# The end of an attention stage: the last batch's maxima in three further rounds, its sums in two parts, and eight units of the output projection in attention's PSUM banks

## The chip, the core and the metric

The kernel runs on one core of one Trainium2 chip, as one launch. The metric is the device time of that launch in microseconds, the median of several executions. Lower is better.

Five engines work side by side, each with its own queue of instructions taken in order: TensorE (PE in the profile, with PEld for its weight loads), VectorE (DVE), ScalarE (ACT), GpSimd (POOL) and SyncE (SP), which here only issues DMAs. All data is float32.

## The reference

Four sub-layers run one after the other over 8 batches of 512 tokens of 256 channels: a sparse attention, a routed feed-forward net, a gated linear attention with its own feed-forward net, and the routed net again. Each is added to its input. The change touches the first only:

```python
q = _split_heads(x @ Wq + bq)          # 16 heads of 16 channels
k = _split_heads(x @ Wk + bk)
v = _split_heads(x @ Wv + bv)
scores = jnp.einsum('bhqd,bhkd->bhqk', q, k) * scale
sparsity = scores.max(axis=-1) - scores.mean(axis=-1)
_, top_idx = jax.lax.top_k(sparsity, U)          # U = 307 of 512 queries
...
attn = jax.nn.softmax(scores_sel, axis=-1)
out_sel = jnp.einsum('bhuk,bhkd->bhud', attn, v)
out = jnp.zeros_like(q).at[bi, hi, top_idx].set(out_sel)
...
return out @ Wo + bo
```

So a query needs its maximum over all keys twice: for the softmax, and to decide whether it is among the 307 of its head whose output is kept. The other 205 give zero.

## The kernel before

**Rounds.** Attention is a loop over 128 steps: batch `b`, channel half `m`, parity `e`, query or key block `k`, 16 steps for each batch. A step handles four heads. The first pass (`max_one`) makes the scores of 128 queries against 512 keys for each of the four heads, in one PSUM bank each, and a DVE reduce (L425) takes the maxima. The second pass (`exp_one`, `weigh`) makes the same scores turned round, ACT takes the exponentials (L437), and four matmuls (L442) sum them with the values into `av`. The second pass runs `LAG = 16` steps behind the first, so in round `n` step `n` of the first pass meets step `n - 16` of the second. Rounds 112 to 127 hold the maxima of the last batch with the exponentials of batch 6; rounds 128 to 143 hold the exponentials of the last batch alone.

**Maxima.** When a group of four steps is done, `place_maxima` (L397 on) transposes and negates its maxima and sends them by eight small DMAs on SP: four into a spare row of `q` (L406), which makes the softmax subtract the maximum, and four into `neg` (L411), which collects the sparsity measure of all 128 batch-head pairs, one on each partition. `top_queries` (L464 on), called when the last maxima are in, copies `neg` into `work` and removes the 205 smallest ones: 26 turns of a DVE `max` that finds eight values and a `match_replace` that strikes them out (L471, L474).

**Sums.** `take` (L449 on) moves `av` to SBUF on ACT, sends the rows that hold the sums of the exponentials to `den` by a DMA on ACT's queue, and adds the outputs into `outC[b]` on POOL.

**The seam.** After the loop, `rden` is the reciprocal of `den` (L615) and `nrm` (L616) is `rden` where the query is kept and zero elsewhere. Sixteen small matmuls (L625) spread `nrm` over the channels of each batch and half, and sixteen DVE multiplications (L628) apply it to `outC`. Then the output projection (`out_projection`, L780) runs in units of one token block `k` and two batches: four matmuls and a DVE addition to the residual `xres` (L784), in the PSUM banks of the stage after. The four units of `k = 0` come first; the twelve others are interleaved with the ten pieces of `route(0)`: statistics of block 0 (L62, L63), a square root on ACT (L64), rows scaled by ACT (L742), their transposes (L752), the router's logits (L810, L820), its softmax and top 4, and the mask `mk`, which goes through DRAM. `routed_ffn(0)` (L904, L912, L913, L885) starts behind it and multiplies by that mask.

**Order.** Each engine's order is fixed when the program is built: a scheduler takes the instructions roughly in the order in which they are written and moves some ahead where it reckons that their inputs are there. A buffer of a pool waits until its last reader is done. The code holds an instruction back by hand with a tiny POOL copy of an element of a late result into the instruction's output (arguments named `late`).

**Banks.** Attention has 8 PSUM banks: three of pool `a_e` (`bank`), four of `a_m` (`bank_m`), one of `a_acc`.

Of the kernel before, what the change touches and what calls it, by code (L numbers as in the profile page):

```python
# [17 lines left out]
P = 128  # L18
NB = 8
# [19 lines left out]
def block_kernel(ctx: ExitStack, tc: tile.TileContext, t: dict, out: bass.AP):  # L39
# [33 lines left out]
    def load_chunked(pool, name, src, eng):  # L73

        n = src.shape[0] // P
        w = pool.tile([P, n, src.shape[1]], F32, tag=name, name=name)
        eng.dma_start(out=w, in_=src.rearrange("(c p) m -> p c m", p=P))
        return w
# [20 lines left out]
    with ExitStack() as outer:  # L99
# [20 lines left out]
        neg = a_out.tile([P, L], F32, name="neg")  # L120
        mx = a_out.tile([P, NB, NG, 4 * 4], F32, name="mx")
        work = a_out.tile([P, L + 8], F32, name="work")
        m8 = a_out.tile([P, 8], F32, name="m8")

        with ExitStack() as inner:
# [4 lines left out]
            def load_heads(name, src, eng):  # L130
                wp = load_chunked(a1, name + "_pad", src, eng)
                w = a1.tile([P, NC2, D], F32, name=name)
                nc.gpsimd.tensor_copy(
                    w.rearrange("p c (h d) -> p (c h) d", d=DH),
                    wp.rearrange("p c (h q) -> p (c h) q", q=32)[:, :, 0:DH],
                )
                return w
# [258 lines left out]
            def place_maxima(b, m, e):  # L396
# [7 lines left out]
                r = b * H + 8 * e + 4 * m  # L404
                for k in range(4):
                    nc.sync.dma_start(  # L406
                        out=q[DH * (1 - e) :: 32, m, bass.ts(k, P)],
                        in_=negT[4 * k : 4 * k + 4, :],
                    )
                for k in range(4):  # L410
                    nc.sync.dma_start(  # L411
                        out=neg[r : r + 4, bass.ts(k, P)], in_=negT[4 * k : 4 * k + 4, :]
                    )

# [49 lines left out]
            def top_queries():  # L464
# [16 lines left out]


            steps = [
                (b, g // 2, g % 2, k) for b in range(NB) for g in range(4) for k in range(4)
# [50 lines left out]
            def place_full(n):  # L535
                while full and full[0][0] <= n:
                    place_maxima(*full.pop(0)[1])

            for n in range(len(steps) + LAG + 1):
                ahead = steps[n] if n < len(steps) else None  # L540
                here = steps[n - LAG] if 0 <= n - LAG < len(steps) else None
# [26 lines left out]
                behind = (here, es) if here is not None else None  # L568
                if ahead is not None and ahead[3] == 3:
                    full.append((n + 2, ahead[0:3]))  # L570
                if n + 1 == len(steps):
                    place_full(n + 2)
                    top_queries()

# [12 lines left out]
                else:  # L587
# [7 lines left out]
                    next(pieces, None)  # L595


        wpool = ctx.enter_context(tc.tile_pool(name="wpool", bufs=1, side="right"))
# [12 lines left out]
        with tc.tile_pool(name="a_tail", bufs=2) as tail:  # L611

            nrm = tail.tile([P, L], F32, tag="nrm", name="nrm", bufs=1)
            rden = tail.tile([P, L], F32, tag="rden", name="rden", bufs=1)
            nc.vector.reciprocal(rden, den)  # L615
            nc.vector.scalar_tensor_tensor(  # L616
                nrm, work[:, 0:L][:, ::-1], REPL, rden, ALU.not_equal, ALU.mult
            )
            for u in range(2):
                for m in range(NC2):  # L620
                    for i in range(4):
                        b = 2 * i + u
                        rows = bass.ts(i, 32)
                        ps = (bank if i % 2 else bank_m)(f"nrm_ps{b}")
                        nc.tensor.matmul(  # L625
                            ps, spread[rows, u, m, :], nrm[rows, :], start=True, stop=True
                        )
                        nc.vector.tensor_tensor(  # L628
                            outC[b][:, m, :], outC[b][:, m, :], ps, ALU.mult
                        )  # L630

# [41 lines left out]
    w_down = load_chunked(wpool, "w_down", t["b_w_downT"], nc.sync)  # L673


    vm = wpool.tile([P, NC2, H], F32, name="vm")
    for c in range(NC2):
        for m in range(NC2):
            mean = vm[:, c, bass.ts(m, H // 2)]
            heads = q_w[:, c, m, 2, :].rearrange("p (h d) -> p h d", d=DH)  # L680
            nc.vector.tensor_reduce(mean, heads, AX.X, ALU.add)
            nc.vector.tensor_scalar(mean, mean, 1.0 / DH, None, ALU.mult)
            nc.vector.tensor_tensor(
                heads, heads, mean.unsqueeze(2).to_broadcast([P, H // 2, DH]), ALU.subtract
            )

# [88 lines left out]
    def out_projection(k):  # L775
# [9 lines left out]

        return [functools.partial(unit, b) for b in range(0, NB, 2)]

# [399 lines left out]
    rest = ctx.enter_context(tc.tile_pool(name="rest", bufs=1, reuse_waits="tile"))  # L1187

    bog = wpool.tile([P, NC2, P], F32, name="bog")
    ones = post.tile([P, P], F32, tag="row", name="ones", bufs=6)  # L1190
# [71 lines left out]
```

## Time and profile before

| | us |
|---|---|
| median of 3 runs (lowest to highest) | 1691.48 (1690.33 to 1694.21) |
| the profiled execution, its own time | 1690.79 |
| its span in the profile | 1689.1 |
| maxima of the last batch, rounds 112 to 127 | 481.9 to 540.6 |
| exponentials of the last batch | 541.9 to 580.3 |
| the 26 turns of `top_queries` | 549.1 to 588.8 |
| first of the spreading matmuls L625 | 593.0 |
| first matmul of the output projection L780 | 605.8 |
| first matmul of `routed_ffn(0)` L904 | 639.5 |
| first read of its mask, L913 | 650.5 |

The granted TensorE clock was 0.987 of full speed over the span. The profile has five parts that count here: busy time of each engine, the chain of work that ended last (followed back from the last instruction to what released it), groups of instructions by line with their mean duration and the idle time ahead of them, a timeline, and a table of busy time by stretches of the span. A duration in a row such as "L425 ... x512 | 328.7, 683" is a total in us and a mean in ns.

### The profile page before, as it was taken

Reading aid. Unit: us, or ns where it says so; the run is one execution under the profiler, and the core shown is the slowest. Engines: PE = TensorE matmul, PEld = TensorE weight load, DVE = VectorE, ACT = ScalarE, POOL = GpSimd, SP = SyncE. Lnnn points to the kernel's source line nnn. Section 1 sums busy time; section 2 is a strip of 40 time slices with the busy share of each in tenths; the row PEclk is TensorE's granted clock in tenths of the full one; section 3 lists DMA queues with packets and bytes.
Section 4 is the critical chain, followed back from the end, with each engine's and each line's share of the span. In section 5 each row is a group of like instructions: output and inputs, shape, how many; then the busy total and the mean of one; then the engine's idle time right before and its main releaser. Section 6 shows DMA issues by size and latency. Waiting matters only on the chain.

```text
span 1689.1 us, 19460 instructions
## 1 busy us (share of the span) xinstructions
PE 1610.8 (95%) x7298; PEld 825.8 (49%) x7298; DVE 975.3 (58%) x2007; ACT 679.7 (40%) x1215; POOL 326.9 (19%) x328
## 2 busy tenths in 40 slices
PE   7999999999999789998899989998999899999999
PEld 3423323323333166665564556545545556666766
DVE  6977777676666984437745465447264632344342
ACT  2466665666566723442253125322512353221010
POOL 3011111011001121114433242224233321000000
PEclk9999999999999989999999999999999999999999
DMA  3100000000000041100000001000000010010100
GB/s 106 39 2 3 3 2 3 2 3 2 2 3 3 24 138 26 26 13 13 0 1 1 0 0 27 0 0 1 0 0 1 1 26 0 13 39 25 48 28 25
DMA packets 23234, 27.55 MB, mean 16 GB/s; under 512 B 4932, under 2 KB 19684, under 8 KB 23140
## 3 DMA queue, kind: packets, MB, share of 16 engines
q1 hardware_dynamic: 22068, 24.74, 5.1%
q10 hardware_dynamic: 1072, 1.57, 0.3%
q8 instruction: 57, 0.93, 0.2%
q14 instruction: 37, 0.30, 0.1%
HBM read 21.19 MB, written 4.33 MB: 15 GB/s over the span
## 4 chain that ended last, share of the span: by engine, by line
PE 78%; DVE 14%; POOL 3%; ACT 2%; issue 1%; DMA 1%; SPq 0%; ACTq 0%; POOLq 0%; DVEq 0%
PE y_ps L885 16%; PE h_ps L904 12%; PE s L433 8%; PE s L422 8%; PE swi_ps L930 7%; PE av L442 7%; PE proj_ps L1012 6%; DVE pr L1044 3%; POOL o L1061 2%; DVE pr L1034 2%; PE ao_ps L780 2%; PE q_ps L316 2%; PE k_ps L316 2%; PE chT_ps L752 2%; PE gla_y L1135 2%; PE v_ps L376 2%
## 5 line engine op out<-in xcount | busy, mean ns | idle before, releaser
L425 DVE TENSOR_REDUCE mx<-s 128x1 f32<-128x512 f32 x512 | 328.7, 683 | 130.2 <-PE s L433 83.1
L437 ACT ACTIVATE e<-s 128x512 f32<-128x512 f32 x512 | 276.1, 599 | 179.1 <-PE s L433 103.5
L422 PE MATMUL s<-k,q 32*128 32x512 f32 x1024 | 299.3, 642 | 3.5 <-ACT k L367 2.8
L433 PE MATMUL s<-q,k 32*128 32x512 f32 x1024 | 294.5, 638 | 0.4 <-DVE mx L425 0.3
L885 PE MATMUL y_ps<-w,h 128*128 128x256 f32 x1024 | 233.4, 383 | 7.6 <-DVE h L913 7.6
L904 PE MATMUL h_ps<-xnT,w 128*128 128x512 f32 x512 | 231.9, 601 | 4.8 <-ACT h L912 4.8
L885 PEld LDWEIGHTS y_ps<-w,h 128*128 128x128 f32 x1024 | 193.6, 192 | 44.6 <-DVE h L913 11.0
L904 PEld LDWEIGHTS h_ps<-xnT,w 128*128 128x128 f32 x512 | 96.1, 193 | 116.1 <-issue 106.1
L442 PE MATMUL av<-e,va 128*32 128x512 f32 (+1 forms) x1120 | 142.0, 568 | 3.8 <-ACT e L437 2.4
L913 DVE TENSOR_TENSOR h<-h,mk 128x512 f32<-128x512 f32 x128 | 94.6, 751 | 84.8 <-ACT h L912 60.1
L930 PE MATMUL swi_ps<-zT,w_gate 128*128 128x512 f32 x256 | 123.1, 603 | 15.0 <-DVE h L939 15.0
L912 ACT ACTIVATE h<-h_ps,b 128x512 f32<-128x512 f32 x96 | 65.6, 685 | 171.4 <-PE h_ps L904 171.2
L930 PE MATMUL swi_ps<-zT,w_up 128*128 128x512 f32 x256 | 123.4, 603 | 10.3 <-ACT h L936 10.3
L890 DVE TENSOR_TENSOR xres<-xres,y_ps 128x512 f32<-128x512 f32 x48 | 32.9, 685 | 172.1 <-PE y_ps L885 157.8
L422 PEld LDWEIGHTS s<-k,q 32*128 32x128 f32 x1024 | 89.8, 184 | 85.8 <-DVE mx L425 55.9
L433 PEld LDWEIGHTS s<-q,k 32*128 32x128 f32 x1024 | 88.2, 183 | 80.7 <-ACT e L437 53.7
L885 PE MATMUL y_ps<-w_down,h 128*128 128x256 f32 x512 | 118.7, 384 | 2.8 <-DVE h L939 2.8
L1012 PE MATMUL proj_ps<-q_w,rT 128*128 128x512 f32 x256 | 117.0, 594 | 0.0
L885 PEld LDWEIGHTS y_ps<-w_down,h 128*128 128x128 f32 x512 | 96.8, 193 | 25.0 <-issue 9.5
L936 ACT ACTIVATE h<-swi_ps 128x512 f32<-128x512 f32 x64 | 37.9, 596 | 148.9 <-PE swi_ps L930 148.8
L1061 POOL TENSOR_TENSOR o<-o,pr 128x512 f32<-128x512 f32 (+2 forms) x56 | 84.7, 1513 | 52.5 <-DVE pr L1044 50.9
L1018 DVE TENSOR_TENSOR gate<-proj_ps,bog 128x128 f32<-128x128 f32 x64 | 18.7, 291 | 125.1 <-ACT made L1017 125.1
(189 smaller groups left out, 1752.8 us busy)
## 6 DMA issues: line engine op xcount, KB each, us to landing
mk<-md SPq DMA_DIRECT2D x32, 256.0 KB
xres<-in_L_attn_a_x SPq DMA_DIRECT2D x8, 512.0 KB
out<-xres SPq DMA_DIRECT2D x16, 256.0 KB
q<-negT SPq DMA_DIRECT2D x128, 2.0 KB
neg<-negT SPq DMA_DIRECT2D x128, 2.0 KB
w<-in_f_w1T SPq DMA_DIRECT2D x1, 1024.0 KB
w<-in_f_w2T SPq DMA_DIRECT2D x1, 1024.0 KB
w_gate<-in_b_w_gateT SPq DMA_DIRECT2D x1, 1024.0 KB
```

Of the source, the lines that this page charges most:

```text
L316: nc.tensor.matmul(ps, w[:, c, bass.ts(m, P)], xnT[:, c, :], start=(c == 0), stop=(c == NC2 - 1),)
L422: nc.tensor.matmul(s, qs[e][rows, m, bass.ts(k, P)], ks[e][rows, m, :], start=True, stop=True)
L425: nc.vector.tensor_reduce(mx[:, b, 2 * e + m, r : r + 1], s, AX.X, ALU.max)
L433: nc.tensor.matmul(s, ks[e][rows, m, bass.ts(kt, P)], qs[e][rows, m, :], start=True, stop=True)
L437: nc.scalar.activation(ex, s, AF.Exp, scale=1.0 / DH**0.5)
L442: nc.tensor.matmul(av[32 * j : 32 * j + 32, queries], va[:, 8 * kt + 4 * m + j, e, :], es[j][:, queries], start=(kt == 0), stop=(kt == 3 a ...
L885: nc.tensor.matmul(y[0][:, bass.ts(i, D)], h[f][:, bass.ts(2 * u + i, P)], w[:, f, :], start=(f == 0), stop=(f == NF - 1),)
L904: nc.tensor.matmul(ps, w1[:, c, bass.ts(f, P)], xT[g][:, c, :], start=(c == 0), stop=(c == NC2 - 1),)
L913: nc.vector.tensor_tensor(hf, hf, mk[g][:, f, :], ALU.mult)
L930: nc.tensor.matmul(ps, w[:, c, bass.ts(f, P)], zT[g][:, c, :], start=(c == 0), stop=(c == NC2 - 1),)
L1012: nc.tensor.matmul(ps, rT[b // G4][:, c, bass.ts(b % G4, P)], q_w[:, c, m], start=(c == 0), stop=(c == NC2 - 1),)
L1061: nc.gpsimd.tensor_tensor(dst, dst, src, ALU.add)
```

## The change

The maxima of the last batch are taken in rounds 112 to 124: in rounds 112, 116 and 120 a second step of the first pass runs behind the regular one, and rounds 125 to 127 have exponentials alone. For the last batch the DMAs into `neg` are issued ahead of those into `q`. `nrm` is made in two parts, first for batches 0 to 5 (96 partitions), then for 6 and 7 (32). Twelve spreading matmuls and multiplications follow the first part; then six units of the output projection for batches 0 to 5 and `k = 0, 1`; then the four spreading matmuls and multiplications of batches 6 and 7; then two units of `k = 2`. These eight units use attention's bank pool `a_e`; ACT copies their result and POOL adds it to `xres`. Eight units remain in `out_projection`, one of which is of `k = 0`. The centering of the `v` weights of the later layer (`vm`, 12 DVE instructions) is written further down. The padded `wq` and `wk` are loaded into two of the buffers that later hold `k`.

```diff
+        def weights_of(batches, late, late_form):
+            rows = slice(16 * batches[0], 16 * batches[-1] + 16)
+            first = slice(rows.start, rows.start + 1)
+            nc.gpsimd.tensor_copy(rden[first, 0:1], late)
+            nc.gpsimd.tensor_copy(nrm[first, 0:1], late_form)
+            nc.vector.reciprocal(rden[rows, :], den[rows, :])
+            nc.vector.scalar_tensor_tensor(
+                nrm[rows, :], work[rows, 0:L][:, ::-1], REPL, rden[rows, :],
+                ALU.not_equal, ALU.mult,
+            )
+
+        def weigh_outputs(batches):
+            picks = itertools.cycle((bank, bank_m))
+            for u in range(2):
+                for m in range(NC2):
+                    for b in batches[u::2]:
+                        strip = bass.ts(b // 2, 32)
+                        ps = next(picks)(f"nrm_ps{b}")
+                        nc.tensor.matmul(
+                            ps, spread[strip, u, m, :], nrm[strip, :], start=True, stop=True
+                        )
+                        nc.vector.tensor_tensor(
+                            outC[b][:, m, :], outC[b][:, m, :], ps, ALU.mult
+                        )
+
+        def out_unit(tail, k, b):
+            y = bank(f"ao_ps{b}")
+            for i in range(2):
+                for m in range(NC2):
+                    nc.tensor.matmul(
+                        y[:, bass.ts(i, D)], outC[b + i][:, m, bass.ts(k, P)],
+                        wo_a[:, m, :], start=(m == 0), stop=(m == NC2 - 1),
+                    )
+            st = tail.tile([P, L], F32, tag="ao", name=f"ao{b}")
+            nc.scalar.copy(st, y)
+            x = xres[:, b : b + 2, k, :]
+            nc.gpsimd.tensor_tensor(x, x, st.rearrange("p (b d) -> p b d", d=D), ALU.add)
...
-                wp = load_chunked(a1, name + "_pad", src, eng)
+                wp = a2.tile([P, NC2, L], F32, tag="k1", name=name + "_pad", bufs=3)
+                eng.dma_start(out=wp, in_=src.rearrange("(c p) m -> p c m", p=P))
...
+                targets = [q[DH * (1 - e) :: 32, m, :], neg[r : r + 4, :]]
+                if b == NB - 1:
+                    targets = targets[::-1]
+                for target in targets:
+                    for k in range(4):
+                        nc.sync.dma_start(
+                            out=target[:, bass.ts(k, P)], in_=negT[4 * k : 4 * k + 4, :]
+                        )
...
+            def all_maxima(step):
+                nonlocal coming
+                coming += 1
+                if step[3] == 3:
+                    full.append((n + 2, step[0:3]))
+                if coming == len(steps):
+                    place_full(n + 2)
+                    top_queries()
...
-                if ahead is not None and ahead[3] == 3:
-                    full.append((n + 2, ahead[0:3]))
-                if n + 1 == len(steps):
-                    place_full(n + 2)
-                    top_queries()
+                if here is not None:
+                    last_exps = es[3][0:1, 0:1]
+                if ahead is not None:
+                    all_maxima(ahead)
+                    if n >= 112 and n % 4 == 0 and coming < len(steps):
+                        ahead = steps[coming]
+                        for i in range(4):
+                            max_one(*ahead, i, bank_m)
+                        all_maxima(ahead)
...
+            weights_of(range(NB - 2), m8[0:1, 0:1], last_exps)
...
-            nc.vector.reciprocal(rden, den)
-            nc.vector.scalar_tensor_tensor(
-                nrm, work[:, 0:L][:, ::-1], REPL, rden, ALU.not_equal, ALU.mult
-            )
-            for u in range(2):
...
+            weigh_outputs(range(NB - 2))
+            last = outC[NB - 3][0:1, 1, 0:1]
+            weights_of(range(NB - 2, NB), last, last)
+            for k in range(2):
+                for b in range(0, NB - 2, 2):
+                    out_unit(tail, k, b)
+            weigh_outputs(range(NB - 2, NB))
+            for b in (0, 2):
+                out_unit(tail, 2, b)
...
-        return [functools.partial(unit, b) for b in range(0, NB, 2)]
+        return [functools.partial(unit, b) for b in range((6, 6, 4, 0)[k], NB, 2)]
```

More of the change, by code (lines that the diff above doesn't have):

```diff
@@ L121, in block_kernel @@
         mx = a_out.tile([P, NB, NG, 4 * 4], F32, name="mx")
+        nrm = a_out.tile([P, L], F32, name="nrm")
+        rden = a_out.tile([P, L], F32, name="rden")
         work = a_out.tile([P, L + 8], F32, name="work")
         m8 = a_out.tile([P, 8], F32, name="m8")
+        def weights_of(batches, late, late_form):
[33 more added lines that the diff above has]
+            nc.gpsimd.tensor_tensor(x, x, st.rearrange("p (b d) -> p b d", d=D), ALU.add)
         with ExitStack() as inner:
@@ L404, in place_maxima @@
                 r = b * H + 8 * e + 4 * m
[L405 to L408, printed above, removed]
-                    )
[L410 to L413, printed above, removed]
+                targets = [q[DH * (1 - e) :: 32, m, :], neg[r : r + 4, :]]
[6 more added lines that the diff above has]
+                        )
             def max_one(b, m, e, k, j, pick):
@@ L537, in place_full @@
                     place_maxima(*full.pop(0)[1])
+            coming = 0
+            def all_maxima(step):
[6 more added lines that the diff above has]
+                    top_queries()
             for n in range(len(steps) + LAG + 1):
-                ahead = steps[n] if n < len(steps) else None
+                ahead = steps[coming] if coming < len(steps) else None
                 here = steps[n - LAG] if 0 <= n - LAG < len(steps) else None
@@ L611, in block_kernel @@
         with tc.tile_pool(name="a_tail", bufs=2) as tail:
[L613 to L616, printed above, removed]
-                nrm, work[:, 0:L][:, ::-1], REPL, rden, ALU.not_equal, ALU.mult
-            )
-            for u in range(2):
[L620 to L630, printed above, removed]
+            weigh_outputs(range(NB - 2))
[7 more added lines that the diff above has]
+                out_unit(tail, 2, b)
     sel = wpool.tile([P, 2 * NBLK], F32, name="sel")
@@ L673, in block_kernel @@
     w_down = load_chunked(wpool, "w_down", t["b_w_downT"], nc.sync)
[L676 to L685, printed above, removed]
     ps_h = ctx.enter_context(tc.tile_pool(name="r_h", bufs=3, space=PSUM))
@@ L1187, in block_kernel @@
     rest = ctx.enter_context(tc.tile_pool(name="rest", bufs=1, reuse_waits="tile"))
+    vm = wpool.tile([P, NC2, H], F32, name="vm")
+    for c in range(NC2):
+        for m in range(NC2):
+            mean = vm[:, c, bass.ts(m, H // 2)]
+            heads = q_w[:, c, m, 2, :].rearrange("p (h d) -> p h d", d=DH)
+            nc.vector.tensor_reduce(mean, heads, AX.X, ALU.add)
+            nc.vector.tensor_scalar(mean, mean, 1.0 / DH, None, ALU.mult)
+            nc.vector.tensor_tensor(
+                heads, heads, mean.unsqueeze(2).to_broadcast([P, H // 2, DH]), ALU.subtract
+            )
     bog = wpool.tile([P, NC2, P], F32, name="bog")
```

## The prediction

> **What bounds the kernel now.** I read the page first: PE is busy 95% of the span and carries 78% of the chain that ended last. What can be won is time in which PE waits. A table of busy time by stretches says where that is (columns: stretch, its length, then busy time and count of PE, PEld, DVE, ACT, POOL, then the granted clock and DMA).
>
> ```profile
> PE 78%; DVE 14%; POOL 3%; ACT 2%; issue 1%; DMA 1%; SPq 0%; ACTq 0%; POOLq 0%; DVEq 0%
> ...
> 481.90:540.60 58.70, 57.85 (x470) 18.45 (x468) 40.67 (x64) 36.93 (x71) 5.60 (x6) 1.00 0.01 3
> 541.90:580.40 38.50, 37.15 (x267) 10.14 (x263) 31.11 (x63) 34.53 (x68) 5.63 (x6) 1.00 0.01 3
> 581.40:593.00 11.60, 0.04 (x4) 0.05 (x4) 11.06 (x20) 1.87 (x2) 3.46 (x10) 0.70 0.44 137
> 593.00:605.80 12.80, 9.03 (x32) 2.73 (x32) 10.74 (x27) 0.00 (x0) 0.00 (x0) 0.77 0.67 166
> 605.80:639.60 33.80, 33.77 (x161) 28.40 (x162) 27.00 (x87) 10.27 (x20) 8.77 (x9) 0.94 0.24 92
> ```
>
> From 581.4 to 593.0 PE does nothing, and up to 605.8 it only feeds 16 multiplications on DVE. From 605.8 it is full again. The chain of waits (start, length, engine, output, line) tells what holds it:
>
> ```profile
> 540.90 1.19 PE s L433 x8
> 542.09 0.27 SPq L406
> ...
> 543.61 0.60 SPq L411
> ...
> 545.53 2.23 DMA neg<-negT
> ...
> 547.85 1.21 DVE work L468
> ...
> 588.77 3.34 DVE rden L615
> 592.11 0.08 DVE prob L838 x2
> 592.19 0.66 DVE nrm L616
> 592.85 0.14 issue
> 592.98 2.10 PE nrm_ps L625 x8
> 595.08 3.44 DVE outC L628 x6
> ...
> 605.83 14.40 PE ao_ps L780 x56
> ```
>
> Last maximum at 540.6, transfers, 41 us of `top_queries`, reciprocal, `nrm`, multiplications, output projection: one serial path on DVE. The exponentials end at 580.3 and the last `av` at 581.4, 11.6 us ahead of `nrm`. So the change is worth what moves the dense matmuls of 605.83 forward.
>
> [...] in windows of 2 us the granted clock is 0.50 from 605 to 609, 0.75 to 611 and 1.00 from there, so the first 4.4 us of the projection ran at half speed and lost 2.2 us. [...] here the order of the built program, read beside the trace, is what I follow for POOL too. [...] in this trace four score matmuls of 32 rows issued from 540.90 take 1.19 us together[...].
>
> **The change, part by part** (times against the profiled execution, 1690.8 us; the median is 0.7 above it).
>
> 1. Maxima. A round without a placement takes 3.5 us (pairs of reduces start at 491.82, 495.30 and 498.83). Three go: -10.5. Each extra step adds four matmuls (1.1 us on PE at least) and four reduces at a stride of 0.645 (2.58 us of DVE at most, 0.4 of it in an idle gap before a pair). The extra matmuls need all four `a_m` banks while two are still being reduced, and the next round's two then wait for those: following bank by bank I get 2.3. Three: +6.9. Maxima end 3.6 earlier (bounds 2.7 and 7.3).
> 2. `neg` first. Four `q` issues, 542.09 to 543.61 in the chain and from 541.23 on SP's timeline, leave the front of the last placement: -2.4. The late `q` rows are read some 30 us on, hidden.
> 3. `top_queries` costs the same. The reciprocal of 96 partitions takes what 128 took (3.34, as its length along a partition is unchanged), and stands before the last strike-out. It waits for a POOL copy of `m8`, +0.2 for the round trip. In the built program that copy stands ahead of `outC` additions of the last batch on POOL, which are held until about 582: 0.77 + 1.27 + 0.77 us, and then the copy that `nrm` waits for. They need some 3.2 us, while DVE has 3.34 + 0.77 to do: hidden. `st` has two buffers for each parity, so ACT isn't held. The last POOL addition ends near 589.7 instead of 586.2, and with it the weight loads start 3.5 later; `vm` is the first to need one (`wvT` near 603) and stands on DVE before the last four multiplications, due at 605: hidden, with 3 us to spare until PE needs them. `nrm` is ready at 592.95 - 3.6 - 2.4 + 0.2 = 587.2.
>  Exponentials: three more rounds alone at 2.4 us (38.4 for 16), +7.2, less 3.6: they end near 583.9, the last `av` at 585.0, still ahead of 587.2.
> 4. Multiplications. First result 2.1 after `nrm` as now, then 0.6 each. The first unit needs the tenth of them: 587.2 + 2.1 + 6.0 = 595.3, its other matmuls run a little before, so the dense stream starts in effect at 594.2, against 605.83: -11.6. In this are four multiplications and the `vm` instructions (12, 1.9 us of busy DVE between them) that no longer stand in the way.
> 5. The four spreading matmuls of batches 6 and 7 now stand inside the dense stream and share strip 3: 0.85 each (a unit of projection streams twice the columns in 1.73 us at full clock), +3.4. The second reciprocal and `nrm` (3.34 + 0.69, from 597 to 601) lie beside six units of projection (10.4 us), their four multiplications beside the two units of `k = 2` (3.45). If that cover went, up to 4 us would show.
> 6. Eight units: same matmuls. ACT copies (0.59 as L452) and POOL additions (1.27 as L460) run inside 1.73 a unit and take 8 x 0.69 from DVE: nothing.
> 7. Clock. PE now idles 2.2 us instead of 11.6 before the spreading matmuls, and five paced ones instead of nine precede the stream. Between 0 and -2.2; I take -1.
> 8. `route(0)` loses cover: 7 units follow the last one of `k = 0` instead of 12 (8.6 us less). From the start of that unit, T, I follow DVE's order in the built program: the shift stands behind four additions, T + 9.2; a table load of 1.28 on ACT now waits for the statistics but is done by then; rows at 0.51 each (six took 3.06) to T + 14, logits T + 16.3, `mT` (7.7 now, 6.5 with fewer additions between) T + 25.5, mask 7.4 later, T + 33, eight multiplications to T + 38. PE has work to the first `y_ps` until T + 33 and to the eighth until T + 36.6. PE waits about 1 at the transposes and 1.3 at `y_ps`: +2.3 (0 to 5).
> 9. Loading the padded weights elsewhere: the third user of those buffers comes long after the copies, nothing.
>
> Sum: -3.6 - 2.4 + 0.2 gives -5.8 for `nrm`; -11.6 for the stream, which contains it; +3.4 - 1.0 + 2.3. Together -6.9, that is 1683.9 for the profiled execution and 1684.6 against the median.
>
> **Rivals.**
>
> - Cheap extras and a warm array (0.13): each extra step hides in DVE's idle 0.9 us a round and costs 1.1, and the stream never runs at half clock. For it: DVE is busy 40.7 of 58.7 us there. Against: only four banks. -6.9 - 3.6 - 1.2 gives 1679.8.
> - The gain is given back in `route(0)` (0.20): the trace has 37.2 us from the end of the last `k = 0` unit (near 613.3) to the first masked product at 650.5, and PE will have about 31 before the first `y_ps`. If the chain keeps that length, the mask comes at T + 38.9 and PE waits 8.2 instead of 2.3: 1690.5. Against: part of the 37 was only the order in which pieces were put between units.
> - Slower (0.10): the same place, longer. Route's statistics, additions and softmax share DVE's queue with eight additions and with route(1)'s statistics, and the table load stands in ACT's. Every us above 33 counts in full; from a wait of 9.2 at the mask (mask at T + 40) the kernel is slower than before. At T + 44, with transposes and softmax each held behind additions, it ends at 1695.6.
> - The change doesn't shorten the maxima because extra steps cost a full round: then -3.1 in place of -6.9, 1688.4. Its chance is inside the forecast's, whose range it bounds above.
>
> **How the numbers follow.** Forecast 0.57, cheap and warm 0.13, given back 0.20, slower 0.10. The forecast's own range is 1681 to 1688. To leave out no more than 2 in 10, I reach to 1679 below and 1691 above, which takes in most of the second and third case. A measurement tells about 0.2%, 3.4 us: faster means below 1688.1. All of the first two and some 0.03 of the third give 0.73 faster; the rest of the third and a little of the fourth give 0.18 same; 0.09 slower.
>
> **What would show it.** Right: last maximum near 537, `work` copied near 541.9, first spreading matmul near 587.2, no PE gap between the tenth multiplication and T near 611.5, and a wait of one to three us at `chT_ps` and `y_ps`. Wrong: DVE's reduces of rounds 112 to 124 in runs without gaps and the last one after 538 (part 1); a POOL releaser ahead of `nrm` (part 3); PE idle at the spreading matmuls of batches 6 and 7 (part 5); the clock at 0.50 after 594 (part 7); a `y_ps` wait on `mk` above 5 us (part 8), which alone would make the forecast fail.

## The result, and the profile after

The median fell from 1691.96 us (5 executions beside it, 1690.33 to 1694.21) to 1685.46 us (5 executions, 1682.0 to 1687.8): ratio 0.9958, 95% interval 0.9941 to 0.9975. The forecast was 1684.6. Run again (e5), the changed kernel took 1686.19 us beside 1692.9: 0.9961, 0.9946 to 0.9975. (Three executions of before beside e5 took 2323 to 9064 us and are left out.)

The profiled executions say less: 1690.79 us before, 1687.8 after, the slowest of its five. They differ by 3.0 us only: before's is one of its faster ones (granted clock 0.987, against 0.984 in the mean of its executions). The text below keeps the two measures apart.

Busy time of the changed kernel by stretches (columns as in the prediction's table: stretch, length, busy time of PE, PEld, DVE, ACT, POOL, then granted clock and DMA):

```profile
482.10:536.20 54.10, 53.35 (x406) 17.61 (x404) 40.01 (x64) 30.75 (x60) 4.84 (x5) 1.00 0.01 3
536.20:583.50 47.30, 45.91 (x337) 12.84 (x337) 40.81 (x79) 41.35 (x82) 6.64 (x9) 1.00 0.01 3
583.50:585.10 1.60, 0.02 (x1) 0.00 (x0) 1.46 (x4) 0.58 (x1) 0.00 (x0) 1.00 0.00 0
585.10:591.90 6.80, 6.78 (x24) 2.99 (x24) 5.62 (x10) 0.00 (x0) 3.45 (x10) 0.61 0.26 54
591.90:604.90 13.00, 13.00 (x50) 10.76 (x49) 8.79 (x13) 2.92 (x5) 6.31 (x7) 0.81 0.85 252
604.90:608.50 3.60, 3.60 (x10) 1.38 (x9) 3.56 (x8) 0.58 (x1) 1.67 (x2) 1.00 0.27 25
608.50:640.00 31.50, 30.77 (x138) 21.19 (x138) 21.49 (x101) 15.23 (x28) 11.31 (x11) 1.00 0.26 98
640.00:660.20 20.20, 18.56 (x63) 11.58 (x62) 8.08 (x11) 7.35 (x13) 3.92 (x3) 0.92 0.21 53
```

PE's hole of 11.6 us is now 1.6 (583.5 to 585.1), and PE is full from 591.9 where it had been from 605.8. Two rows show what was paid: 604.9 to 608.5 holds ten matmul records in 3.6 us (eight are the four spreading matmuls of batches 6 and 7), and in the last row PE is idle for 1.64 us and the mean clock is 0.92.

The chain of waits of the changed kernel for the same place (start, length, engine, output, line):

```profile
580.10 0.18 POOL rden L132
...
580.31 3.30 DVE rden L134
583.61 0.68 DVE work L519
...
584.38 0.70 DVE nrm L135
...
585.12 6.87 PE nrm_ps L147 x24
591.99 12.94 PE ao_ps L160 x48
604.93 3.62 PE nrm_ps L147 x8
608.55 3.67 PE ao_ps L160 x16
```

The reciprocal starts at 580.31 instead of 588.77, the first spreading matmul at 585.12 instead of 592.98. Part of this lies at the front of `top_queries`, as DVE's timeline shows (start, length, line, operation, in brackets DVE's idle time before it and what ended it), first before, then after:

```profile
547.85 1.20 DVE L468 COPY work<-neg 128x512 f32<-128x512 f32 x1 [7.28 <-DMA neg<-negT]
```

```profile
540.72 0.43 DVE L513 COPY work<-neg 128x512 f32<-128x512 f32 x1 [4.54 <-DMA neg<-negT]
```

From the last maximum to the copy DVE waits 4.54 us instead of 7.28, and the copy takes 0.43 instead of 1.20: before, a POOL addition from 547.49 to 548.76 ran beside it.

### The profile page after: what moved, and what is told of

Its sections match the earlier page's. It is cut to its first block, busy times and chain, and to the rows that moved or that the text cites. A ratio compares the mean times of both kernels' runs of the same rounds, so it can differ in the third digit from the quotient of the medians.

```text
span 1686.1 us, 19496 instructions
## 1 busy us (share of the span) xinstructions
PE 1618.9 (96%) x7298; PEld 827.7 (49%) x7298; DVE 976.2 (58%) x2001; ACT 684.6 (41%) x1223; POOL 337.8 (20%) x340
## 4 chain that ended last, share of the span: by engine, by line
PE 78%; DVE 12%; POOL 3%; issue 3%; ACT 3%; DMA 1%; ACTq 0%; POOLq 0%; DVEq 0%
PE y_ps L928 16%; PE h_ps L947 11%; PE s L467 8%; PE s L478 8%; PE swi_ps L973 7%; PE av L487 7%; PE proj_ps L1055 6%; DVE pr L1087 3%; POOL o L1104 2%; DVE pr L1077 2%; PE q_ps L362 2%; PE chT_ps L794 2%; PE k_ps L362 2%; PE gla_y L1178 2%; PE v_ps L422 2%
## 5 line engine op out<-in xcount | busy, mean ns | idle before, releaser
L478 PE MATMUL s<-q,k 32*128 32x512 f32 x1024 | 291.0, 638 | 0.5 <-DVE mx L470 0.3
L973 PE MATMUL swi_ps<-zT,w_up 128*128 128x512 f32 x256 | 123.3, 603 | 10.3 <-ACT h L979 10.3
L933 DVE TENSOR_TENSOR xres<-xres,y_ps 128x512 f32<-128x512 f32 x48 | 32.9, 685 | 172.1 <-PE y_ps L928 157.8
```

Source lines behind the costliest of these rows:

```text
L478: nc.tensor.matmul(s, ks[e][rows, m, bass.ts(kt, P)], qs[e][rows, m, :], start=True, stop=True)
L973: nc.tensor.matmul(ps, w[:, c, bass.ts(f, P)], zT[g][:, c, :], start=(c == 0), stop=(c == NC2 - 1),)
```

## Two measures for one experiment

Executions of one kernel differ by several us, and the granted clock goes with it. In the profiles every stretch at clock 0.50 is a multiple of 3.41 us, such as one of them (654.8 to 658.2 in after), three (586.5 to 596.8 in after) or seven (586.7 to 610.6 in e1); the last one is cut by the end of the record. Before took 1695.0 us in the mean of ten executions at a clock of 0.980 and 1690.3 in seventeen at 0.988; the changed kernel 1690.1 in two at 0.985 and 1683.5 in five at 0.991. So each kernel below has two numbers: its median, and a distance inside one profile, from a maximum of the loop near 460 us (the 427th of the 512, before anything differs) to the first `y_ps` addition (L933; `y_ps` is the output of `routed_ffn(0)` in PSUM, which DVE adds to `xres`). The same work lies between these two points in every kernel, the filling matmuls and a few of `y_ps` apart. A third column has the distance from there to the last `y_ps` addition, in which no kernel's instructions differ but those of e7, e8, e9 and e12 by the place of four POOL additions. The kernels were measured in five groups, each with before beside it, whose median lay between 1691.6 and 1692.9: across groups the ratios compare, not the medians.

| | median us | ratio to before | loop to first `y_ps` addition | from there to the last |
|---|---|---|---|---|
| before | 1691.96 | 1 | 203.11 | 1022.66 |
| after | 1685.46 | 0.9958 (0.9941 to 0.9975) | 200.58 | 1022.02 |
| e1 maxima and `neg` alone | 1693.4 | 1.0003 (0.9995 to 1.0011) | 203.61 | 1024.64 |
| e2 seam alone | 1699.73 | 1.0038 (1.0025 to 1.0051) | 209.45 | 1026.77 |
| e3 without further rounds | 1696.08 | 1.0020 (1.0012 to 1.0028) | 207.43 | 1024.69 |
| e4 units back | 1693.39 | 1.0003 (0.9995 to 1.0011) | 203.44 | 1025.29 |
| e5 after again | 1686.19 | 0.9961 (0.9946 to 0.9975) | 199.04 | 1024.30 |
| e6 array kept busy | 1690.07 | 0.9980 (0.9973 to 0.9987) | 200.92 | 1024.71 |
| e7 `b2` later | 1686.19 | 0.9959 (0.9944 to 0.9973) | 199.13 | 1024.29 |
| e8 e6 and e7 together | 1689.41 | 0.9977 (0.9969 to 0.9985) | 202.64 | 1024.26 |
| e9 `b2` held | 1686.41 | 0.9960 (0.9948 to 0.9972) | 196.94 | 1024.74 |
| e10 e1, array kept busy | 1693.06 | 1.0001 (0.9993 to 1.0010) | 203.58 | 1025.48 |
| e11 e6, `vm` held | 1686.45 | 0.9967 (0.9956 to 0.9977) | 196.57 | 1023.71 |
| e12 mixed and held | 1686.04 | 0.9965 (0.9951 to 0.9979) | 194.50 | 1024.56 |

The last column moves by up to 4.8 us with hardly an instruction changed: the pauses of the later stages are followed by a step at 0.50 in one profile and not in the other. The time at 0.50 in this part is 23.9 us in before and after, 34.1 in e5, 37.6 in e2. A single profile can't tell 2 us of the total; it can tell what happens at one place.

The mean granted clock was 0.982 to 0.984 in e1 to e4, as in before (0.984); it was 0.988 in after, e5 and e7 together, and 0.986 to 0.989 in the others.

## The experiments: the change taken apart

**e1, the maxima alone.** The kernel before, with the further rounds and `neg` first, nothing else:

```diff
+                if b == NB - 1:
+                    targets = targets[::-1]
...
+                    if n >= 112 and n % 4 == 0 and coming < len(steps):
+                        ahead = steps[coming]
+                        for i in range(4):
+                            max_one(*ahead, i, bank_m)
+                        all_maxima(ahead)
```

> The kernel before with the three further rounds and the neg transfers first, and nothing else of the change. My theory: the two halves of the change need each other. Here the single reciprocal of all 128 partitions must wait for the last den transfer, and the exponentials end later than before (three more rounds of them alone): last av near 583, den landed near 586, first spreading matmul near 590 instead of 593.0, so only 2.5 to 3 us are gained. Rival (the maxima are the whole gain, and the rest of the change is worth nothing): first spreading matmul near 585.5 and 6.5 to 7.5 us gained.

Measured: no gain, 1.0003. The figures of both theories were wrong. DVE's timeline of e1 shows where it went:

```profile
587.20 3.35 DVE L628 RECIPROCAL rden<-den 128x512 f32<-128x512 f32 x1 [6.03 <-POOL st L458]
...
593.51 4.27 DVE L641 TENSOR_TENSOR outC<-outC,nrm_ps 128x512 f32<-128x512 f32 x7 [2.23 <-PE nrm_ps L638]
601.02 0.48 DVE L694 TENSOR_REDUCE vm<-q_w 128x8 f32<-128x128 f32 x2 [3.25 <-DMA q_w<-in_b_wvT]
```

`top_queries` was done at 581.17, but the one reciprocal of all 128 pairs needs the sums of the last batch, and those come late, since the last exponentials had moved back by some 2 us. The chain of waits of e1 names it:

```profile
584.44 1.79 DMA den<-st
...
586.40 0.77 POOL st L458
...
587.25 1.27 POOL outC L459
...
594.76 6.05 DMA q_w<-in_b_wvT
```

DVE idles 6.03 us, and only some 2 of the gain arrive at `nrm`. Then the second bracket: weight loads of the later stages start behind POOL's last `outC` addition (now 588.5), the `v` weights land at 600.8, and `vm` stands on DVE with nine multiplications behind it. It waits 3.25 us; before it waited for nothing (599.25). The rest of the gain is gone there, and the projection starts at 607.6. From the first spreading matmul to the projection e1 takes 16.2 us, before 12.9: the wait accounts for the difference. e1 with `vm` further down was not run, so what the further rounds would bring without this wait is open.

**e10, the same with the array kept busy.** In e1 the clock was 0.50 from 586.7 to 610.6. Was that the cause? Twelve filling matmuls of the full array before the spreading ones, two after each four:

```diff
+            keep_busy(12, bank)
             for u in range(2):
                 for m in range(NC2):
+                    if u or m:
+                        keep_busy(2)
```

> The kernel before with the further rounds and neg first (as e1, which gained nothing: 1693.4), and filling matmuls of the full array: twelve before the first spreading matmul, two after each four. Theory (e1's gain of some 2.3 us at the first spreading matmul was lost to seven steps of 3.41 us at half clock, of which 7 us lie in the dense projection from 603.5 to 610.6): clock 1.00 until the projection, dense stream 3.5 us of work ahead of e1, median 1689.5 to 1690.5. Rival (e1's loss isn't the clock, but the same order of work behind it): 1692.5 to 1694.

The time is the rival's, 1.0001, but the run doesn't do what its theory asks for. The clock stayed at 1.00 only to 597.4 and was 0.50 from there to 611.1, so the projection started in the cold again. Its first stretch at 0.50 (columns as above), in before, in e1 and in e10:

```profile
605.83:610.01 4.18, 4.18 (x10) 3.38 (x11) 1.10 (x3) 0.00 (x0) 0.00 (x0) 0.50 1.02 413
```

```profile
607.62:610.57 2.95, 2.95 (x7) 2.41 (x8) 0.74 (x2) 0.00 (x0) 0.00 (x0) 0.50 0.88 343
```

```profile
606.01:611.06 5.05, 5.04 (x12) 4.06 (x13) 2.60 (x8) 0.00 (x0) 0.00 (x0) 0.50 0.71 216
```

So e10 can't rule the clock out. The lines do: in e1 only 2.95 us of the projection were cold (not the 7 that the theory took; up to 607.6 PE was still at the spreading matmuls), which is less than in before, and DVE's first seven multiplications took 4.27 us in both. So the clock took nothing from e1 there that before didn't lose as well. `vm` waited in e10 too (2.70 us, to 601.09). The weight load stays as the reason; the trace shows it, no experiment with e1.

**e3 and e2, the seam without the maxima.** e3 is the changed kernel without the further rounds, e2 also without `neg` first:

```diff
-                    if n >= 112 and n % 4 == 0 and coming < len(steps):
-                        ahead = steps[coming]
-                        for i in range(4):
-                            max_one(*ahead, i, bank_m)
-                        all_maxima(ahead)
```

> The change without the three further rounds, all else kept. My theory: everything behind the last maximum moves back by what the rounds gave (4.4 us by the two traces), so the gain over the kernel before falls from about 6.5 to about 2 us; the first spreading matmul is near 589.5. Rival (the rounds only move the wait to the exponentials, which then end later): no more than 1 us is lost against the changed kernel.

> The change without the three further rounds and with neg behind q as before: only the sums in two parts, the eight units in attention's banks and vm further down. My theory: nrm comes where it came before (593), the dense stream starts near 600 instead of 605.8, but it holds four spreading matmuls (3.6 us), and PE then waits 2 to 4 us in route(0) and at the first y_ps for lack of cover: 0 to 2 us gained. Rival (the early units that fill PE's idle time are the gain): 5 us or more gained.

Both are slower than before, by 0.2% and 0.4%, which neither their theories nor their rivals had. e3's `nrm` (DVE's timeline):

```profile
588.07 1.49 DVE L135 SCALAR_TENSOR_TENSOR nrm<-work,rden 96x512 f32<-96x512 f32 x1
```

It is the instruction that took 0.69 in before. A POOL addition into `outC` ran from 587.75 to 589.01 beside it. In after the same addition ran from 586.99, when `nrm` was done (0.70 in the chain above).

From the common point of the loop to the start of the dense stream e2 needs 142.4 us, e3 138.9, before 146.4, after 132.3. So the seam alone starts PE 4.0 us earlier (e2), and yet the first `y_ps` addition comes 6.3 later: from there on it is 10.3 us longer than before (e3 11.8, after 11.6). That is the price of the new seam, and it is the reason why a part of the change is worse than none. `neg` first is worth 2.0 between the two points (e2 to e3), the further rounds 6.9 (e3 to after). By the ratios the further rounds are worth some 10 us; that the excess over 6.9 is the clock (0.983 in e3, 0.988 in after) would fit, but is not shown.

**e4, the units back.** All sixteen units of the projection behind the last multiplication, as before, `vm` held back by POOL:

```diff
-            for k in range(2):
-                for b in range(0, NB - 2, 2):
-                    out_unit(tail, k, b)
             weigh_outputs(range(NB - 2, NB))
-            for b in (0, 2):
-                out_unit(tail, 2, b)
```

> The change with the eight early units put back into the later projection (16 units there, route(0) has its twelve covering units again), and vm held behind block 0 of the residual. Maxima, neg order and two-part sums are kept. My theory: PE idles through the second reciprocal, and the dense stream starts near 602 instead of 592, but holds no spreading matmuls and no waits in route(0): 3.5 to 5 us gained over the kernel before, so the early units are worth about 2 us. Rival (the early units give back all they win, through lost cover): as fast as the changed kernel or faster. Second rival (the early units are the main gain): not faster than the kernel before.

Nothing gained: 1.0003, the case of the second rival. PE's timeline of e4:

```profile
584.93 6.87 PE L147 MATMUL nrm_ps<-nrm,spread 32*128 32x512 f32 x24 [1.57 <-DVE nrm L135]
597.95 7.19 PE L147 MATMUL nrm_ps<-nrm,spread 32*128 32x512 f32 x8 [6.14 <-DVE nrm L135]
605.92 6.35 PE L817 MATMUL ao_ps<-wo_a,outC 128*128 128x256 f32 x18 [0.78 <-DVE outC L150]
```

The second reciprocal and `nrm` leave PE idle for 6.14 us, and the four spreading matmuls of batches 6 and 7, one after the other in strip 3, take 7.19 at half clock (the clock was 0.50 from 586.5 to 610.4) where they take 3.62 in after. Dense work starts at 605.9, as before. So the six units in between are what makes the two parts pay: they cover the second reciprocal and `nrm`, and the clock comes back to 1.00 under them. They are not the gain alone: e2 and e3 have them and lose.

## The experiments: what the change had to pay

**e5, the changed kernel again,** as the base of the next three.

> The changed kernel itself, once more, as the base of the three beside it. Both theories: 1685.5 us within 1.5 for the median. What it adds: TensorE's granted clock changes in steps of 3.41 us in every trace so far, so the number of such steps at 0.50 may differ between executions of one kernel; if it does, single executions lie 1.7 us apart per step, and the anchors in the trace, not the time of one execution, have to carry a comparison.

Its profiled execution has the array warm where after's had it cold. The granted clock at the start of the dense stream (same columns as above), after first, then e5:

```profile
590.00:592.00 2.00, 2.00 (x8) 0.41 (x2) 2.00 (x4) 0.00 (x0) 0.00 (x0) 0.50 0.84 188
592.00:594.00 2.00, 2.00 (x5) 1.64 (x6) 1.65 (x4) 0.00 (x0) 0.30 (x2) 0.50 1.02 390
594.00:596.00 2.00, 2.00 (x6) 1.55 (x6) 2.00 (x1) 0.21 (x1) 0.00 (x0) 0.50 1.08 372
```

```profile
590.00:592.00 2.00, 1.93 (x8) 0.51 (x8) 2.00 (x4) 0.00 (x0) 1.43 (x8) 1.00 0.06 6
592.00:594.00 2.00, 1.80 (x8) 1.06 (x6) 2.00 (x5) 0.00 (x0) 0.00 (x0) 1.00 0.94 240
594.00:596.00 2.00, 1.90 (x9) 1.70 (x10) 1.65 (x4) 0.59 (x1) 0.55 (x3) 1.00 0.96 347
```

Same program, same idle time of 1.6 us ahead of the spreading matmuls. On the grid of 3.41 us, which can be read off the clock changes in each trace, the idle time fell into one step in after and was cut in two by a step's edge in e5. It was followed by 0.50 from 586.5 to 596.8 in after, which took in the first 4.86 us of the dense stream, and by 1.00 up to 606.8 in e5.

**e6, the array kept busy.** If the cold start costs, filling should help:

```diff
+        def keep_busy(n, pick=acc):
+            ps = pick("warm_ps")
+            for _ in range(n):
+                nc.tensor.matmul(ps[:, 0:D], ident, wo_a[:, 0, :], start=True, stop=True)
...
+                    if fill:
+                        keep_busy(fill)
...
-            weigh_outputs(range(NB - 2))
+            keep_busy(4, bank)
+            weigh_outputs(range(NB - 2), 1)
```

> The changed kernel with seven or so filling matmuls (full array, result unused): four between the last av and the first spreading matmul, one after each three spreading matmuls of the six batches. Theory (32-row matmuls don't hold the clock; in the trace of after the clock is 0.50 from 586.5 to 596.8, and the dense projection, from 591.9, runs at half speed in 4.9 us of it): the clock stays 1.00, the dense stream does the same work 2.4 us sooner, and the median falls by 2 to 2.5 us against the run of after beside it. Rival (DVE's multiplications pace this stretch, the clock costs nothing): the clock changes and the time stays within 0.7 us, or rises by up to 1.5 us since the filling matmuls stand in the way of the spreading ones.

The clock was 1.00 until 605.4, as the theory had it, and the median rose by 3.9 us against e5: neither case. DVE's timeline of e6:

```profile
592.99 3.35 DVE L134 RECIPROCAL rden<-den 32x512 f32<-32x512 f32 x1 [0.35 <-POOL rden L132]
600.26 0.29 DVE L1246 TENSOR_REDUCE vm<-q_w 128x8 f32<-128x128 f32 x1 [3.92 <-DMA q_w<-in_b_wvT]
600.57 1.69 DVE L135 SCALAR_TENSOR_TENSOR nrm<-work,rden 32x512 f32<-32x512 f32 x1
```

The scheduler had put one `vm` instruction ahead of the second `nrm`. It waited 3.92 us for the `v` weights, PE ran out of dense work at 601.4 and stood still for 0.99 us, and behind the four spreading matmuls that followed, all in one 32-row strip of the array, the clock was 0.50 from 605.4 to 612.3.

**e11, the same with `vm` held** behind the sixteenth multiplication:

```diff
+            vm = wpool.tile([P, NC2, H], F32, name="vm")
+            nc.vector.tensor_copy(
+                vm[0:1, :, :: H // 2],
+                outC[NB - 1][0:1, 1, 0:4].rearrange("o (c m) -> o c m", m=NC2),
+            )
```

> e6 with the DVE instructions of vm held behind the last of the sixteen multiplications. In e6 they stood ahead of the second nrm and waited for the v weights, which landed at 600.2; PE had run out of dense work, then did 32-row matmuls alone, and the clock fell to 0.50 from 605.4 to 612.3. Theory (the weight load has become the bound in e6): the second spreading matmuls start by 600.5 instead of 602.4, at most one step at 0.50 before 615, median 3 to 4.5 us below e6 (1690.1), that is 1685.6 to 687.1 with 1600 added where it is left out, about level with e5. If the filling is worth its 2.4 us as well, 1683 to 1685. Rival (the filling matmuls themselves delay the spreading ones): still above 1688.5.

(The upper figure of the first range stands for 1687.1.) Measured: 3.6 us below e6 in the median (2.2 by the ratios), level with e5. There is no step at 0.50 from the loop to the first `y_ps` addition, but the second spreading matmuls started at 602.59, not 600.5: the dense stream of 48 records began at 592.14 and took 10.5 us. So the weight load had cost e6 its time, and the filling keeps the clock; in the median it brings nothing over e5. That the array is warm at this place in part of the changed kernel's executions anyway, as in e5's profile, would explain it, and is not shown for the median.

**e7, `b2` later.** Ahead of the first `y_ps` matmuls DVE multiplies eight pieces by the mask. In after this took 7.05 us for 4.9; the last two ran beside POOL's additions of `b2`, a bias, to `xres` for `route(1)`. These additions were to move:

```diff
-            for u in range(2):
-                xs = tokens(k, G4 * g + 2 * u)
-                nc.gpsimd.tensor_tensor(
-                    xs, xs, b2.unsqueeze(1).to_broadcast([P, 2, D]), ALU.add
-                )
+            if key != (1, 1):
+                add_b2(k, g)
...
+        if key == (1, 1):
+            for g in range(2):
+                add_b2(k, g)
```

> The changed kernel with the four POOL additions of b2 in route(1) moved behind its mask, out of the stretch in which DVE masks the first eight pieces of routed_ffn(0). Theory (the POOL additions stretch DVE's multiplications beside them, 7.05 us for eight in after, and the pause of PE at y_ps then costs a step of 3.41 us at clock 0.50): eight multiplications in 5.0 us, PE at y_ps waits less than 0.7 in all, no step at 0.50 between 650 and 665, and the median falls by 2.5 to 4 us. Rival (the mask's arrival sets it, the multiplications would be late anyhow): less than 1 us.

Nothing moved, in the median or in the trace: POOL's timeline of e7 has them at the old place.

```profile
650.57 1.30 POOL L838 TENSOR_TENSOR xres<-xres,b 128x512 f32<-128x512 f32 x1 [8.16 <-ACT row L784]
652.19 1.35 POOL L838 TENSOR_TENSOR xres<-xres,b 128x512 f32<-128x512 f32 x1 [0.32 <-ACT row L784]
```

Written later, they were taken ahead again by the scheduler, since their inputs were there. The run says nothing about the theory. Nor does **e8**, the edits of e6 and e7 together, whose additions stand at 654.12 and 655.74 beside the multiplications: it is e6 once more (1689.41 and 1690.07).

> Both edits of the two kernels before this. If the two costs are independent, the sum: 4.5 to 6.5 us below after, near 1680. Rival (route(0)'s chain, from the start of the last unit of k = 0 on, has to fit under the work of PE: what the array gains ahead of it is waited for again at y_ps, because mask and multiplications don't come earlier): no more than the better one of the two alone, with PE's idle time at chT_ps or y_ps longer by what the dense stream gained.

**e9, `b2` held** by a value, so that no scheduler can bring it forward:

```diff
+        if key == (1, 1):
+            nc.gpsimd.tensor_scalar(
+                b2[0:1, 0:1], ready["late"][0:1, 0:1], 0.0, b2_0, ALU.mult, ALU.add
+            )
+            for g in range(2):
+                add_b2(k, g)
```

> e7 left the additions where they were: the scheduler brought the two of route(1) back to 650.6 and 652.2, beside DVE's multiplications. Here they are held by an element of the eighth masked piece (times zero, added to b2), so they can't start before it. Theory (POOL stretches the last two multiplications from 0.69 to 1.75 us each, 2.1 us, and PE pauses for them at y_ps): eight multiplications in 5.0 us instead of 7.05, no pause of PE between 650 and 656, and the median falls by 1.6 to 3.5 us against 1686.2 of e5. Rival (PE would wait at another place anyway): y_ps starts earlier, and the time comes back within 50 us; less than 1 us.

DVE's multiplications and PE's busy time and clock at that place, first in after, then in e9:

```profile
647.15 7.05 DVE L956 TENSOR_TENSOR h<-h,mk 128x512 f32<-128x512 f32 x8
...
652.00:654.00 2.00, 0.70 (x2) 0.30 (x2) 2.00 (x2) 0.16 (x1) 1.35 (x1) 1.00 0.00 0
654.00:656.00 2.00, 1.75 (x5) 1.46 (x6) 0.20 (x1) 0.00 (x0) 0.00 (x0) 0.70 0.00 0
656.00:658.00 2.00, 2.00 (x6) 1.58 (x5) 0.00 (x0) 0.00 (x0) 0.00 (x0) 0.50 0.00 0
```

```profile
646.88 4.91 DVE L969 TENSOR_TENSOR h<-h,mk 128x512 f32<-128x512 f32 x8
...
652.00:654.00 2.00, 2.00 (x11) 1.77 (x11) 0.00 (x0) 0.00 (x0) 1.92 (x3) 1.00 0.01 4
654.00:656.00 2.00, 2.00 (x11) 1.77 (x10) 0.00 (x0) 0.00 (x0) 2.00 (x3) 1.00 0.00 0
656.00:658.00 2.00, 2.00 (x13) 1.75 (x12) 1.86 (x6) 0.00 (x0) 2.00 (x3) 1.00 0.00 0
```

In after PE is busy for 0.70 of 2 us, and then runs at half clock for one step of 3.41 us: 1.64 us of idle time and 1.71 us of speed lost. In e9 both are gone, and the first `y_ps` addition is 3.6 us nearer to the loop. The mechanism at this place is shown. The median isn't lower than e5's (ratio 0.9960 against 0.9961): 1686.41, with a granted clock of 0.986 in the mean of its five executions.

**e12, three edits together:** `b2` held, `vm` held, and the two units of `k = 2` between the spreading matmuls of batches 6 and 7.

```diff
-            weigh_outputs(range(NB - 2, NB))
+            weigh_outputs(
+                range(NB - 2, NB), [functools.partial(out_unit, tail, 2, b) for b in (0, 2)]
+            )
...
+                        if between:
+                            between.pop(0)()
```

> The changed kernel with three edits: b2 held as in e9, vm held as in e11, and the two projection units of k = 2 put between the four spreading matmuls of batches 6 and 7 (one after the first, one after the second). No filling. Theory (the 4.1 us that e9 gained at the first y_ps addition are real, and its median of 1686.4 is due to more steps at half clock behind it in its few executions, mean clock 0.986 against 0.988 in the 21 executions of the changed kernel's order): first y_ps addition 4 us earlier than after counted from the loop, h*mk eight in 5.0 us, no step at 0.50 from 605 to 665, median 1682 to 1684.5. Rival (what is gained at y_ps is always given back within the later stages): 1685.5 to 1687.5.

The trace does what the theory says, save one step at 0.50 (611.4 to 614.9, behind a pause of 1.22 us that PE now makes for the last multiplication): 194.50 us to the first `y_ps` addition, 6.1 less than after and 4.5 less than e5. The median is the rival's: 1686.04, mean of six executions 1685.9, against 1686.4 in 21 executions of the changed kernel's order (after, e5, e7). Its executions lie between 1684.5 and 1687.1, those 21 between 1682.0 and 1690.4. No version here is shown to beat the changed kernel.

## Why the prediction was right, and where its sum was not

**What held.** Each part of the front: DVE's path is shortened, two parts of sums are needed to use it, `top_queries` costs the same, the first parts of `nrm` and projection pay.

1. Maxima, -3.6: against e3 the last maximum comes 4.9 us earlier. An extra step costs (10.5 - 4.9) / 3 = 1.9 us, not 2.3.
2. `neg` first, -2.4: the wait for the copy is 2.7 shorter. Another 0.8 comes from the copy itself (0.43 instead of 1.20), beside which no POOL addition runs any more; this was not in the sum.
3. `nrm` at 587.2: it was 585.1. The reciprocal took 3.35 us for 96 partitions and for 32, 3.34 for 128 before. POOL's copy stood where it was said, hidden. `vm` waited 3.75 us in after, until 602.09, and its multiplications ended at 609.5, while PE had work: hidden, as said, with little to spare. e1 and e6 show this wait on the path as soon as PE or the order of DVE gives it no cover. In these runs it is the wait that comes next.
4. Dense stream, -11.6: it started 13.9 earlier, at 591.9. Its first 4.86 us, to 596.8, ran at half clock (2.4 lost).
5. Strip of batches 6 and 7, +3.4: 3.6. The four matmuls of this one strip took 3.62 us one after the other, at clock 1.00, where before's four score matmuls of four strips took 1.19 together; the prediction's 0.85 each was an estimate. The cover for the second reciprocal held. e4 prices it: without it PE is idle for 6.14 us, where the prediction said up to 4.
6 and 9. ACT copies, POOL additions and the padded weights, 0: right for PE. But beside the additions three of DVE's small `vm` instructions took 1.04 to 1.26 us instead of 0.16 to 0.28.
8. `route(0)`, +2.3: PE's idle time is 0.20 at the transposes (`chT_ps`), 0.53 at the transposes for the mask (`mT`) and 1.64 at `y_ps`, 2.4 together. The sum was right, its reason at `y_ps` was not. The mask's first product came at T + 35.1 (T = 612.04), 2 us later than reckoned; but what PE waited for were the seventh and eighth product, at 1.75 us each beside POOL (e9).

**What failed** is step 7, the clock, "-1 (0 to -2.2)", as a term and as a kind. In the profiled pair the start of the stream brought nothing: 2.1 us lost in 4.18 at half clock before, 2.4 lost in 4.86 after. And a step at 0.50 behind the pause at `y_ps` cost 1.71 that no step of the sum had. That less idle time ahead of the stream would spare it the half clock was an estimate. In after, 0.50 followed two steps of 3.41 us in which PE had stood still for only 1.6 (583.1 to 586.5, and 651.4 to 654.8), and the same 1.6 us ahead of the spreading matmuls was followed by 1.00 in e5.

Over all executions it is the other way: the mean granted clock is 0.9836 in 103 executions of before and 0.9884 in the 21 of the changed kernel's order, some 16 us less at 0.50, or 8 us of speed. That is worth up to 8 us, more than the whole gain, if PE was busy in all of it, and nothing where PE was idle; e10, whose clock rose to 0.986 without a gain, shows that it can be nothing. Where both kernels have executions at the same mean clock (0.985 to 0.988, 38 of before and 10 of the changed one), the changed kernel is 1.5 to 3.5 us faster, which agrees with the profiled pair. So an estimate from these means is that about half of the measured 6.5 us is work moved forward and the rest goes with fewer steps at 0.50. The estimate is rough, since it sets warm executions of before against cold ones of the changed kernel. e1 to e4, parts of the change, don't have the higher clock; after and the kernels built on it have it. Through which pauses is not shown.

So the closeness of 1684.6 to 1685.46 owes much to luck. The sum of -6.9 was made for the profiled pair, and there 13.9 us are gained at the front, of which 2.4 are left at the first `y_ps` addition (662.56 to 660.20) and 3.0 at the end. Of the 11.5 that go, 3.6 are the strip, 2.4 idle time, 1.7 clock at `y_ps`, 0.3 clock at the start, and 1.0 comes because the router's eight matmul records now run in two groups of 1.05 us instead of one of 1.06. That places 9 of 11.5; the rest I could not place. Two small figures of the prediction don't come out of its lines: at the start of the projection before, 4.18 us and not 4.4 ran at half clock, and its rival of full rounds sums to -3.3 and not -3.1.

**The rivals.** The warm array (0.13) is there in e5's profile, and its first `y_ps` addition is only 1.5 us nearer to the loop than after's. The gain given back in `route(0)` (0.20) is true in part: 3.35 us at `y_ps`, taken away by e9. The slower case (0.10) needed the mask at T + 40; it was there at T + 35. An extra step at the cost of a full round did not happen.

**Open:** why e9 and e12, 3.6 and 6.1 us ahead of after at the first `y_ps` addition, have no lower median. In their profiles the stages behind take 1024.7 and 1024.6 us, with 37.6 and 34.1 us at 0.50, in after's 1022.0, with 23.9. In e5's they take 1024.3, with 34.1; but e5's profiled execution is the slowest of its eight, so the pair e5 and e12 says little about the medians.

## What to carry to other kernels

When two serial paths of similar length meet (here the selection of queries and the last sums), shortening one can give nothing, as in e1, and a version that does half can be slower than none, as e2 and e3: take a change apart before keeping or rejecting it, and ask at each cut which load or which queue is due next. An instruction that waits for a load delays what stands behind it on its engine (by 3.92 us in e6), so place it by what stands behind it. Read places in the trace, not totals of single profiles, where pauses and the clock's grid move the total by more than the change (the last column of the table by up to 4.8 us, while the profiled pair differs by 3.0).

## What the hardware showed that was not expected

- Some DVE instructions took longer beside a POOL `tensor_tensor`: the copy into `work` 1.20 us instead of 0.43, `nrm` 1.49 (e3) and 1.69 (e6) instead of 0.69, a masking multiplication 1.75 instead of 0.69. Others kept their pace: in after the `max` and `match_replace` of `top_queries` (0.69 and 0.68 beside the addition at 549.44, as without one), the reciprocal (3.35 beside the addition at 581.10, 3.34 in before with none) and the seam's multiplications, one of whose inputs is in PSUM: twelve in 7.26 us with a POOL addition beside them (586.99 to 588.25), and twelve in 7.26 in e3 with none. What decides it is not shown.
- A stretch of 32-row matmuls was followed by the half clock in one profile and not in another, and the two lay differently on the grid of 3.41 us. In e5 the clock fell to 0.50 at 606.8, behind a step that lay wholly in the strip's matmuls (603.4 to 607.2); in after the strip (604.9 to 608.5) shared each step with dense work, and the clock stayed at 1.00. PE was busy throughout both.
- Stages with the same instructions took 1022.0 us with 23.9 us at 0.50 in them (after), 1024.3 with 34.1 (e5) and 1026.8 with 37.6 (e2).
